# Attention with rational scores: new places for norm, block end and queries, and another instruction order in key tiles 23 to 31

## The chip, the cores and the metric

The kernel runs on one core of one Trainium2 chip. The metric is the device time of one execution in microseconds (us), the median over repeated runs. Five engines work side by side, each in its own order: TensorE (PE, matrix products into PSUM), VectorE (DVE), ScalarE (ACT, functions such as logarithm and exponential), GpSimd (POOL) and SyncE (SP, which issues DMA transfers). [...]

## The reference

The input x is 4 x 128 x 64 x 64. A first layer (group norm, convolutions, a selective scan) adds its result to x; the change does not touch it. The second layer treats each of the four images as 4096 tokens of 128 channels, normalises each token, and adds an additive attention; a recurrent layer follows. The attention is:

```python
q = jnp.einsum('bld,ud->blu', x, Wt)
k = jnp.einsum('bld,ud->blu', x, Wx)
beta = jnp.tanh(q[:, :, None, :] + k[:, None, :, :] + bh)
alpha = jnp.einsum('bsju,u->bsj', beta, Wa[:, 0]) + ba[0]
alpha = jnp.tanh(alpha)
alpha = jax.nn.softmax(alpha, axis=-1)
c_r = jnp.einsum('bsj,bjd->bsd', alpha, x)
```

So every query meets every key through 32 hyperbolic tangents, weighted by Wa and summed.

## The kernel before

The stage in question is `_rational`. It doesn't evaluate 32 tangents for each pair of query and key. The 32 units are put into six small groups, and the weighted sum of the tangents of one group is a quotient of two sums over products of exponentials. Both sums are matrix products of a table for the keys, F, with a table for the queries, E (lower sum, the denominator) or cE (upper sum, the numerator). The tables are exponentials of projections (`keys`, `queries`; `weigh` makes cE from E).

**Tiles and blocks.** For each of the 4 batches (images) there are 8 query blocks of 512 queries, 32 blocks in all. Within a block the loop runs over 32 key tiles of 128 keys, number jt. A tile's scores go to A[:, jt, :], 128 keys by 512 queries. When all tiles of a block are there, a seam follows: tanh and exp over A in four parts (PARTS), the first weighted sums over the values (`weighted`, accumulated in one PSUM bank, `ct`), and tile 0 of the next block, computed ahead without ScalarE (`ahead`, `direct`, with VectorE's reciprocal). So all blocks but the first start their loop at tile 1. Where a batch ends, the next batch's key table is made in the seam as well (`all_keys`), and the transposed values (`turn`, eight of them) in the loop of the block that follows.

**One tile.** The six groups are served as three units, A, B1 and B2, of two groups each. Each unit needs:
- d: the lower sums, two matmuls into two PSUM banks (`lower`; called dA, dB1, dB2 here; two buffers of two banks in all). A uses rows 0 to 63 and 64 to 127 of TensorE, B1 rows 0 to 31 and 32 to 63, B2 rows 64 to 95 and 96 to 127.
- n: the upper sums, two matmuls into two numerators' banks (`upper`; nA, nB1, nB2).
- ln and ex: ScalarE takes the logarithm of the lower sums and then the exponential of its negative, which gives the reciprocals (lines 1231 and 1232).
- x: VectorE multiplies them with the upper sums, one multiply for each bank (`times`, line 1227).

Then POOL adds the products of B1 to those of A (a1, line 1349) and those of B2 (a2, line 1334), and VectorE adds the two halves of the result into A (f, line 1346). n and x of B2, a2 and f of a tile are issued in the next tile's iteration. The products of A live in the pool `ra` (three buffers), those of B1 and B2 in the pool `rb` (four buffers of one unit).

**Order.** Each engine is handed its instructions in the order in which the Python code issues them. In one iteration TensorE gets dA(jt), nB2(jt-1), dB1(jt), nA(jt), dB2(jt), nB1(jt); ScalarE ln and ex of A, B1 and B2 in turn; VectorE xB2(jt-1), xA(jt), xB1(jt), f(jt-1); POOL a2(jt-1), a1(jt).

**Extra steps.** Other work is put between the tiles by number: `between[jt]` runs at the end of iteration jt, `middle[jt]` within it, after a2.
- The last 12 weighted sums of the block before run in `middle`, tiles 2 to 13.
- The end of the block before (`closing`) has seven steps at CLOSE_AT: the copy of `ct` to SBUF, a matmul for the softmax denominators, four quarter reciprocals, and the last step: a matmul, a VectorE multiply, a POOL add to the residual `xr` (line 1264) and the store on SP.
- The norm of a part of the next batch has four steps at NORM_AT: centre (matmul, VectorE subtract), square (ScalarE), rate (matmul, ScalarE ln and exp, lines 71 and 72) and scale (POOL multiply, line 1164). The blocks of batches 0 to 2 have it, those of the fourth batch do not.
- The two halves of the next block's query table come at QUERIES_AT: a matmul, an exponential, and a maximum on VectorE.

PSUM holds two buffers for the lower sums (four banks), three numerators' banks (`pn`, taken in turn; also used by turns and the norm), and one bank `ct` for the weighted sum, the block end and the queries (`pw`).

## Time and profile before

| | |
|---|---|
| median of 3 runs | 11600.68 us (11594.8 to 11604.92) |
| the profiled execution's own time | 11599.52 us |
| its span, first to last instruction | 11597.8 us |
| granted TensorE clock, mean | 0.935 |
| busy share PE, DVE, ACT, POOL | 89%, 78%, 82%, 74% |
| first ScalarE table load of the attention loop, and the last one that follows a seam | 4001.83 us, 11137.38 us |
| a1, a2, f: mean of one | 2656 ns, 2362 ns, 749 ns |

A row of a group or of the timeline names the line of the program, the engine, the operation, the tile written and the tiles read, and the shape as partitions by elements. In the timeline the two numbers ahead are start and duration in us; what stands in brackets at the end is how long the engine was idle before, and what ended that. `pd` are the banks of the lower sums, `pn` those of the upper sums, `ra` and `rb` the products. A matmul in fp32 has two records (passes), so a unit of two matmuls has four. PEld is the loading of weights.

### The profile page before, as it was taken

How to read it: one execution, taken by the hardware profiler on the slowest of the kernel's cores; microseconds unless marked ns; L12 is line 12 of the kernel's file. 1: busy time of each engine (PE TensorE's matmuls, PEld its weight loads, DVE VectorE, ACT ScalarE, POOL GpSimd, SP SyncE). 2: the span in 40 equal slices, each digit the busy share in tenths (PEclk: the TensorE clock that was granted, in tenths of full speed). 3: DMA queues.
4: the chain of work that ended last, by engine and by line, in shares of the span. 5: the costliest groups of instructions: out<-in, count | busy, mean ns of one | idle time of the engine just before them, and what ended most of it. 6: DMA issues, size and time to landing. Idle time of an engine off the chain costs nothing.

```text
span 11597.8 us, 111820 instructions
## 1 busy us (share of the span) xinstructions
PE 10265.4 (89%) x36210; PEld 3139.3 (27%) x36210; DVE 8992.9 (78%) x10066; ACT 9467.7 (82%) x10209; POOL 8626.5 (74%) x3703
## 2 busy tenths in 40 slices
PE   6787787778777699999999999999999999999997
PEld 2121121122111132232233223323323233333334
DVE  4998899889889677777777777777777777777773
ACT  3556656656555599999999999999999999999995
POOL 3999889889889677767766776767677767776773
PEclk8898898888888799999999999999999999999998
DMA  4888778778778300000000000000000000000001
GB/s 118 189 182 195 169 179 192 178 173 190 180 169 194 85 1 3 6 3 4 6 3 3 3 6 3 3 3 6 3 3 3 6 2 3 3 4 3 2 3 60
DMA packets 225333, 737.77 MB, mean 64 GB/s; under 512 B 41105, under 2 KB 41937, under 8 KB 223713
## 3 DMA queue, kind: packets, MB, share of 16 engines
q1 hardware_dynamic: 221760, 729.96, 26.7%
q8 instruction: 286, 4.69, 0.2%
q14 instruction: 311, 2.54, 0.1%
q10 hardware_dynamic: 2976, 0.58, 0.0%
HBM read 612.95 MB, written 117.44 MB: 63 GB/s over the span
## 4 chain that ended last, share of the span: by engine, by line
PE 50%; ACT 10%; DVE 3%; issue 3%; POOL 0%; DMA 0%; POOLq 0%; DVEq 0%; SPq 0%; ACTq 0%
PE pn L1212 26%; PE pd L1212 16%; PE ct L1360 4%; ACT A L1384 4%; ACT A L1385 2%; DVE rb L1227 2%; ACT rb L1231 1%; ACT rb L1232 1%; PE ct L1134 1%; ACT ra L1231 1%; PE vy L1559 1%; DVE A L1346 0%; PE ct L1262 0%; PE pn L56 0%; ACT L1384 0%
## 5 line engine op out<-in xcount | busy, mean ns | idle before, releaser
L1212 PE MATMUL pn<-cE,F 32*128 32x512 f32 (+1 forms) x12288 | 4691.2, 651 | 189.9 <-DVE rb L1227 86.0
L1212 PE MATMUL pd<-E,F 32*128 32x512 f32 (+1 forms) x12288 | 3481.5, 649 | 20.4 <-DVE ra L1239 15.5
L1349 POOL TENSOR_TENSOR ra<-ra,rb 128x1024 f32<-128x1024 f32 x993 | 2637.0, 2656 | 1077.5 <-DVE rb L1227 1077.3
L1227 DVE TENSOR_TENSOR rb<-rb,pn 128x512 f32<-128x512 f32 x3972 | 2566.0, 681 | 960.0 <-ACT rb L1232 369.5
L626 POOL TENSOR_TENSOR dBu<-dtdu,bbcc 128x1024 f32<-128x1024 f32 x1024 | 2397.9, 2367 | 217.8 <-DMA dtdu<-ddd 158.8
L1334 POOL TENSOR_TENSOR ra<-ra,rb 128x1024 f32<-128x1024 f32 x993 | 2345.6, 2362 | 228.4 <-DVE rb L1227 123.9
L1232 ACT ACTIVATE rb<-rb 128x1024 f32<-128x1024 f32 x1986 | 2099.5, 1057 | 62.9
L1231 ACT ACTIVATE rb<-pd 128x1024 f32<-128x1024 f32 x1986 | 2004.6, 1009 | 112.5 <-PE pn L1212 84.9
L1212 PEld LDWEIGHTS pn<-cE,F 32*128 32x128 f32 (+1 forms) x12288 | 1367.1, 186 | 2553.9 <-DVE rb L1227 1386.2
L668 PE MATMUL py<-h,gather 128*32 128x512 f32 x4096 | 1300.7, 701 | 471.3 <-POOL h L651 359.7
L1227 DVE TENSOR_TENSOR ra<-ra,pn 128x512 f32<-128x512 f32 x1986 | 1288.2, 683 | 528.1 <-PE pn L1212 325.0
L1212 PEld LDWEIGHTS pd<-E,F 32*128 32x128 f32 (+1 forms) x12288 | 933.2, 186 | 1646.9 <-issue 820.7
L621 ACT ACTIVATE pa<-dtdu,a_neg 128x1024 f32<-128x1024 f32 x1024 | 1145.2, 1118 | 53.1 <-DVE h L641 32.1
L651 POOL TENSOR_TENSOR h<-h,bbcc 128x1024 f32<-128x1024 f32 x384 | 911.7, 2374 | 346.0 <-ACT carry L649 336.5
L641 DVE TENSOR_TENSOR_SCAN pa<-pa,carry,dBu 128x1024 f32<-128x1024 f32 x480 | 1124.5, 2343 | 23.1 <-ACT pa L621 11.3
L1232 ACT ACTIVATE ra<-ra 128x1024 f32<-128x1024 f32 x993 | 1049.7, 1057 | 31.4
L1360 PE MATMUL ct<-A,xT 128*128 128x512 f32 x2048 | 1052.3, 642 | 8.8 <-ACT A L1385 8.8
L1231 ACT ACTIVATE ra<-pd 128x1024 f32<-128x1024 f32 x993 | 1001.3, 1008 | 31.7 <-PE pd L1212 26.4
L649 ACT COPY carry<-pa 128x1 f32<-128x1 f32 x640 | 102.5, 160 | 1044.2 <-DVE h L648 1042.2
L1346 DVE TENSOR_TENSOR A<-ra 128x512 f32<-128x512 f32 x993 | 743.3, 749 | 115.9 <-POOL ra L1334 115.8
L648 DVE TENSOR_TENSOR h<-pa,bbcc 128x1024 f32<-128x1024 f32 x640 | 783.8, 1225 | 59.0 <-PE py L668 0.9
L641 DVE TENSOR_TENSOR_SCAN h<-pa,carry,dBu 128x1024 f32<-128x1024 f32 x288 | 675.0, 2344 | 171.0 <-PE py L668 141.1
(291 smaller groups left out, 8740.9 us busy)
## 6 DMA issues: line engine op xcount, KB each, us to landing
bbcc<-bcd SPq DMA_DIRECT2D x1024, 256.0 KB, 6.9
dtdu<-ddd SPq DMA_DIRECT2D x1024, 256.0 KB, 7.2
ddd<-dd SPq DMA_DIRECT2D x64, 1024.0 KB, 5.1
src<-src SPq DMA_DIRECT2D x64, 512.0 KB, 8.3
xs<-in_x_dram SPq DMA_DIRECT2D x16, 512.0 KB, 7.5
src<-xs SPq DMA_DIRECT2D x16, 512.0 KB, 3.0
bcd<-bc SPq DMA_DIRECT2D x64, 128.0 KB, 2.0
src<-xsT SPq DMA_DIRECT2D x16, 512.0 KB, 5.4
```

What stands on the lines that cost most here:

```text
L621: nc.scalar.activation(dA, its[m].DT[r][:, 0, :], AF.Exp, scale=a)
L626: nc.gpsimd.tensor_tensor(dBu, its[m].DT[r][:, 1, :], its[m].BC[q][:, 0, :], ALU.mult)
L641: nc.vector.tensor_tensor_scan(to[:, step], dA[:, step], live.pop(("dBu", u))[:, step], 0.0 if m % nch == 0 else its[m - 1].carry[:, col : ...
L651: nc.gpsimd.tensor_tensor(h, h, cc, ALU.mult)
L668: nc.tensor.matmul(it.y[to, c], gather, live["h", v][:, c], start=False, stop=(q == QS - 1))
L1212: nc.tensor.matmul(ps[a], F[lo:hi, i, jt * P : (jt + 1) * P], side[lo:hi, i, :], start=True, stop=True)
L1227: nc.vector.tensor_tensor(r[:, a, :], r[:, a, :], ns[a], ALU.mult)
L1231: nc.scalar.activation(r, d, AF.Ln, scale=LOWER)
L1232: nc.scalar.activation(r, r, AF.Exp, scale=-1.0)
L1334: nc.gpsimd.tensor_tensor(rA_, rA_, rB2_, ALU.add)
L1349: nc.gpsimd.tensor_tensor(rA, rA, rB1, ALU.add)
L1360: nc.tensor.matmul(ct, xT[:, jt, :], A[:, jt, :], start=(jt == 0), stop=(jt == JT - 1))
```

## The change

Every step of a tile gets a number of its own, and all steps of a block, with the extra steps, are sorted by number and issued in that order. For tiles up to 22 the numbers (EARLY_STEPS) give the order from before. From tile 23 on (LATE_STEPS) they give another one: ScalarE runs lnA, lnB1, exA, lnB2 and then one exponential over B1 and B2 together (exB, 128 x 2048); TensorE runs, from tile to tile, nB1(jt-1), dB2(jt), nB2(jt-1), dA(jt+1), nA(jt), dB1(jt+1); VectorE xB1(jt-1), f(jt-2), xB2(jt-1), xA(jt); POOL a1(jt-1), a2(jt-1).

For that, the products of B1 and B2 share one buffer of the pool `rb` (now three buffers of two units). The bank that was `ct` becomes the fourth of the numerators' banks from tile 23 on; up to there three are taken in turn as before, and the fourth serves weighted sum, block end, queries and, newly, the rate of the norm. The extra steps all end before: block end at tiles 13 to 18, norm at 14 to 20, queries at the ends of tiles 20 and 21. The norm's square is kept in the A tile of key tile 31, which is free then; the exponential of the rate is written to the PSUM bank, and the scale is a VectorE multiply that reads it there, where it was a POOL multiply. The sums f of tiles 30 and 31 are issued in the seam, behind the first `direct` of the next block's tile 0.

```diff
-CLOSE_AT = (14, 16, 17, 18, 19, 20, 22)
-NORM_AT = (15, 17, 19, 20)
-QUERIES_AT = (24, 26)
+LATE = 23
+CLOSE_AT = (13.45, 14.45, 14.95, 15.95, 16.95, 17.95, 18.95)
+NORM_AT = (14.95, 16.95, 19.95, 20.45)
+QUERIES_AT = (20.95, 21.95)
+EARLY_STEPS = dict(
+    dA=0.00, dB1=0.10, nA=0.20, lnA=0.21, exA=0.22, xA=0.23, dB2=0.30, nB1=0.31, lnB1=0.40, exB1=0.41,
+    xB1=0.42, a1=0.44, lnB2=0.50, exB2=0.51, nB2=1.05, xB2=1.12, a2=1.13, f=1.43,
+)
+LATE_STEPS = dict(
+    dA=-0.44, dB1=-0.23, lnA=-0.12, lnB1=-0.04, exA=0.26, dB2=0.37, lnB2=0.50, nA=0.74, xA=0.81, exB=0.84,
+    nB1=1.11, xB1=1.38, nB2=1.42, xB2=1.49, a1=1.75, a2=1.88, f=2.46,
+)
...
-    rb = ctx.enter_context(tc.tile_pool(name="nrb", bufs=4))
+    rb = ctx.enter_context(tc.tile_pool(name="nrb", bufs=3))
-    psN = ctx.enter_context(tc.tile_pool(name="npsN", bufs=3, space=PSUM))
-    psW = ctx.enter_context(tc.tile_pool(name="npsW", bufs=1, space=PSUM))
+    psN = ctx.enter_context(tc.tile_pool(name="npsN", bufs=1, space=PSUM))
...
+    turns = {"taken": 0, "banks": 3}
     def pn():
-        return psN.tile([P, QB], F32, name="pn", tag="pn")
+        i = turns["taken"] % turns["banks"]
+        turns["taken"] += 1
+        return psN.tile([P, QB], F32, name=f"pn{i}", tag=f"pn{i}")
     def pw():
-        return psW.tile([P, QB], F32, name="ct", tag="ct")
+        return psN.tile([P, QB], F32, name="pn3", tag="pn3")
...
+    def norm_within(xn, cols, A):
...
+        def square():
+            nc.scalar.activation(A[:, JT - 1, :], xc, AF.Square)
+        def rate():
+            held["ps"] = ps = pw()
+            nc.tensor.matmul(ps, k.avg, A[:, JT - 1, :], start=True, stop=True)
+            nc.scalar.activation(A[:, JT - 1, :], ps, AF.Ln, bias=k.eps5)
+            nc.scalar.activation(ps, A[:, JT - 1, :], AF.Exp, scale=-0.5)
+        def scale():
+            nc.vector.tensor_tensor(xc, xc, held["ps"], ALU.mult)
...
+    def four():
+        return rb.tile([P, 4, QB], F32, name="rb", tag="rb")
+    def pair():
+        return ra.tile([P, 2, QB], F32, name="ra", tag="ra")
+    def steps(jt, F, E, cE, A, first):
...
+        when = EARLY_STEPS if jt < LATE else LATE_STEPS
...
+        if jt >= LATE:
+            go["exB"] = lambda: exp(h["rb"])
+        else:
+            go["exB1"] = lambda: exp(halves("B1"))
+            go["exB2"] = lambda: exp(halves("B2"))
...
+        return [(jt + when[name] + (JT if name == "f" and jt >= JT - 2 else 0), f) for name, f in go.items()]
...
+            between.append((LATE - 0.05, lambda: turns.update(banks=4)))
+            for jt in range(start, JT):
+                between += steps(jt, F, E, cE, A, first if jt == start else None)
+            between.sort(key=lambda e: e[0])
+            for _, go in between[:-2]:
+                go()
+            sums = [go for _, go in between[-2:]] if more else []
...
                 if step == 0:
-                    held["A"], held["B1"] = lower("A", F, 0, E), lower("B1", F, 0, E)
-                    held["A"] = direct(held["A"], upper("A", F, 0, cE), ra, "ra")
+                    dA, held["dB1"] = lower("A", F, 0, E), lower("B1", F, 0, E)
+                    held["A"], held["B"] = pair(), four()
+                    direct(held["A"], dA, upper("A", F, 0, cE))
+                    for go in sums:
+                        go()
...
-                    between.setdefault(22 + c, []).append(lambda xT=xT, xn=xn, c=c: turn(xT, xn, c))
+                    between.append((21.85 + c, lambda xT=xT, xn=xn, c=c: turn(xT, xn, c)))
```

## The prediction

> **What bounds the kernel now.** I read the page's busy shares first, then the stretches by engine, then the timeline of single tiles. The attention stage runs from 4044 to about 11378 us: 32 query blocks of 31 key tiles (32 in the first), a seam after each.

> ```profile
> PE 10265.4 (89%) x36210; PEld 3139.3 (27%) x36210; DVE 8992.9 (78%) x10066; ACT 9467.7 (82%) x10209; POOL 8626.5 (74%) x3703
> L1231 ACT ACTIVATE rb<-pd 128x1024 f32<-128x1024 f32 x1986 | 2004.6, 1009 | 112.5 <-PE pn L1212 84.9
> L1231 ACT ACTIVATE ra<-pd 128x1024 f32<-128x1024 f32 x993 | 1001.3, 1008 | 31.7 <-PE pd L1212 26.4
> ```

> The second and third rows are the logarithms; what follows the second bar is idle time of ScalarE before them. Next, two stretches: one whole block without its seam, and three tiles in it.

> ```profile
> 6350.98:6548.66 197.68, 194.08 (x777) 58.23 (x776) 145.29 (x225) 188.99 (x192) 155.88 (x64) 0.98 0.01 5
> 6475.00:6496.50 21.50, 19.20 (x70) 5.43 (x69) 15.92 (x23) 16.53 (x18) 15.31 (x8) 0.84 0.03 10
> ```

> Columns are PE, PEld, DVE, ACT, POOL and the granted clock. ScalarE is busy 189.0 of 197.7 us in the block, yet 16.5 of 21.5 in the three tiles. So ScalarE sets the pace except in one place. Its pace in an undisturbed tile:

> ```profile
> 6074.71 1.00 ACT L1231 ACTIVATE ra<-pd 128x1024 f32<-128x1024 f32 x1
> 6075.75 1.06 ACT L1232 ACTIVATE ra<-ra 128x1024 f32<-128x1024 f32 x1
> 6076.71 1.00 ACT L1231 ACTIVATE rb<-pd 128x1024 f32<-128x1024 f32 x1
> 6080.72 1.00 ACT L1231 ACTIVATE ra<-pd 128x1024 f32<-128x1024 f32 x1
> 6096.16 1.91 ACT L1385 ACTIVATE A<-A 128x2048 f32<-128x2048 f32 x1
> 6097.97 3.69 ACT L1384 ACTIVATE A<-A,b_a 128x4096 f32<-128x4096 f32 x1
> ```

> A tile is 6.00 us (6074.71 to 6080.72). An exponential starts 1.04 after the logarithm it needs (1.00 long); the next, independent instruction starts 0.96 after the exponential (1.06 long). Independence is worth an overlap of 0.09, dependence costs 0.04. The 2048-wide exponential takes 1.91, its successor starts after 1.81.

> The bad place, first how a good tile looks, then a block's tile 21 to 22:

> ```profile
> 6007.16 0.70 PE L1212 MATMUL pn<-cE,F 32*128 32x512 f32 x2
> 6007.24 0.70 PE L1212 MATMUL pd<-E,F 32*128 32x512 f32 x2
> 6007.51 0.69 DVE L1346 TENSOR_TENSOR A<-ra 128x512 f32<-128x512 f32 x1
> 6007.69 0.59 PE L1212 MATMUL pn<-cE,F 32*128 32x512 f32 x2
> 6007.73 2.68 POOL L1349 TENSOR_TENSOR ra<-ra,rb 128x1024 f32<-128x1024 f32 x1 [1.49 <-DVE rb L1227]
> 6010.49 2.36 POOL L1334 TENSOR_TENSOR ra<-ra,rb 128x1024 f32<-128x1024 f32 x1
> ...
> 6482.27 2.35 POOL L1349 TENSOR_TENSOR ra<-ra,rb 128x1024 f32<-128x1024 f32 x1
> 6482.35 2.81 DVE L1346 TENSOR_TENSOR A<-ra 128x512 f32<-128x512 f32 x1 [0.42 <-POOL ra L1334]
> 6485.82 1.85 PE L1212 MATMUL pn<-cE,F 64*128 64x512 f32 x2 [2.06 <-DVE rb L1227]
> 6489.78 1.02 ACT L1231 ACTIVATE rb<-pd 128x1024 f32<-128x1024 f32 x1 [3.17 <-PE pn L1212]
> 6493.42 1.02 ACT L1231 ACTIVATE ra<-pd 128x1024 f32<-128x1024 f32 x1 [1.53 <-PE pd L1212]
> ```

> In the good tile f (L1346) starts 0.22 before the POOL add a1 and takes 0.69. In the bad one a1 starts 0.08 before f, and f takes 2.81: it ends 0.54 after a1 does. xB2 is queued behind f, the numerators' banks behind xB2, TensorE behind the banks. TensorE idles 2.06, its next pair takes 1.85 where such a pair takes 1.12 (clock 0.84 in that stretch), and ScalarE loses 3.17 + 1.53 = 4.70. The cause stands a tile earlier: POOL's scale of the norm (L1164, 1.27 us) comes between a1 and a2, so a2 ends late and a1 follows at once.

> **Part 1, tiles 23 to 31 (LATE_STEPS).** ScalarE's order becomes lnA, lnB1, exA, lnB2, exB, with one 2048-wide exponential. Start to start: lnA 0.92, lnB1 0.92, exA 0.97 (each with the overlap), lnB2 1.03 (exB needs it), exB 1.82: 5.66 instead of 6.00. Do the others keep up? Put lnA(j) at 0.
> - TensorE. A unit of two matmuls takes 1.06 (6006.10 to 7.16). Now nB2+dB1 and dB2+nB1 run as pairs on different row groups, four slots a tile. In the new order dB2, nB2, dA, nA, dB1, nB1, equal row groups follow each other, and only nB1 with the next dB2 can overlap. dB2 waits for lnA (1.01), so dB2 at 1.1, nB2 2.16, dA 3.22, nA 4.28, dB1 5.34 to 6.40; lnB1 of the next tile wants it at 6.58: 0.18 to spare. Own loop: 5 x 1.06 + 0.08 = 5.38.
> - VectorE: six multiplies and f, at 0.64 and 0.6 apart: 4.5. xA follows nA (5.34), xB1 nB1 (7.45 to 8.7), then f, xB2 9.35 to 10.6.
> - POOL: from the end of xB1, 0.22 + 2.68 + 0.08 + 2.36 = 5.34 to the end of a2; the next f is safe if that is under the period: 0.32 to spare (0.66 now).
> - Four numerators' banks: nA reuses those of nB1(j-1), free at 8.7 - 5.66 = 3.0, before 4.28. Three fours of rb live until a2, 13.9, against reuse at 17.9. No wait.

> I take 5.70, for one handover of 0.04. In three blocks turns stand in these tiles (one more PE slot of 0.7, so 6.0: no gain). 29 x 9 x 0.30 = 78 us. Bounds: ScalarE with every overlap, 3 x 1.01 + 1.06 + 1.91 - 5 x 0.09 = 5.55 (117 us); below that nothing in the rows allows.

> The order on TensorE deserves a look. In the rows above, dB1's first pass starts 0.08 after nB2's while nB2's second pass waits until 0.53: a later matmul on free row groups passes waiting ones. [...]

> **Part 2, tiles 13 to 22.** Take, denominator, reciprocals, end, norm and queries move up; each issues the same matmuls, activations and VectorE work as before, and the ScalarE part (square 0.54, rate 1.24, two E of 0.5) costs the same elsewhere. On SP the end's store stands ahead of the next block's xr and xn loads (6495.19, 6497.19, 6497.56); all three come four tiles earlier and are needed 20 tiles later. Scale leaves POOL: 1.27 gone there, 0.68 more on VectorE (the row of a multiply with a PSUM operand), which has a quarter of its time free. Without that cover it would cost 24 x 0.68 = 16. The exponential of the rate writes PSUM: 0.63 before; no row shows that direction, 0.5 to 0.7 either way is 24 x 0.1 = 2 us, taken as 0.

> The end's POOL add (1.27) remains. It alone also makes f lose, as the fourth batch shows, whose blocks have no norm: f took 2.85 at 9936.00 and ScalarE lost 2.29. After the change the add is at 18.95 in every block. In the 24 blocks with a norm, the rate's 1.24 us on ScalarE and one matmul follow a tile later, at 19.95, just where f is blocked: the 2.2 us delay of xB2 meets ScalarE 1.24 later, and TensorE idles 0.7 (1.78 before the row at 9939.51, less the rate's 1.06). I keep 0.5 per block (bounds 0 and 2.3, from 2.29).
> Total of the stall now: 84.9 + 26.4 = 111. Fourth batch: 8 x 2.29 = 18, stays. The rest, 93, becomes 24 x 0.5 = 12: gain 81.

> **Part 3, the seam.** f(30) and f(31) move behind the first direct reciprocals. ScalarE fills 31.7 us there (table load 6092.83 to lnA at 6124.54) with tanh and exponentials; the last tanh needs f(31) 19.6 after the load. xB2(31) ends 2.6 after it, weigh 0.9, direct 8.1, two f 1.3: 13. Cost 0; without this cover 31 x 1.3 = 40. Tiles 1 to 12 keep their order: 0.

> **Sum**, against the profiled execution (11599.5, span 11597.8; median of the runs 11600.7): 11599.5 - 78 - 81 = 11440.

> **Rivals.**
> 1. The stall only changes its cause: the end's add does in each block what the scale did, f 2.8 long, TensorE slow. For it: the fourth batch. Against: there no rate follows. Only part 1 is left: 11599.5 - 78 = 11521.
> 2. TensorE becomes the bound in the late tiles: no overlap at all, 6 x 1.06 = 6.36 a tile; 261 x 0.36 = +94, less 81: 11612. For: three numerators of four now stand behind an equal row group. Against: the 0.08 above.
> 3. Slower: POOL loses the race in tiles 23 to 31. From the point where a1 and a2 need more than the period (0.32 away), f is blocked in each tile: f 2.85, xB2 1.28, a2 2.36, handovers: 6.55 a tile, and the gain of the shorter exponential cannot be used. 261 x 0.55 = +144, less 81: 11662. Against: a blocked f delays xA and xB1 too, which lets POOL catch up, and VectorE's other multiplies (0.68 beside POOL) don't collide.

> **How the numbers follow.** Forecast 0.68, rival 1 0.18, rival 2 0.06, rival 3 0.08. Range: low end 11599.5 - 117 - 93 = 11390, a little under it for the rows' rounding, 11380; high end rival 1 with the slower late tile (44): 11555, taken as 11545. About 0.2% (23 us) is what a measurement can tell. Faster: forecast and rival 1, 0.86; within: rival 2, 0.06; slower: rival 3, 0.08.

> **What would show it.** Distance of lnA in tiles 23 to 30: 5.7; over 5.8 with waits on PE speaks for rival 2. Mean of f (0.749 now): near 0.70 if the collisions go; over 0.9 is rival 3. Idle of the logarithms on PE (111 now): near 30; if it stays over 90, rival 1. I am wrong if the seam waits for f(31), or tiles 13 to 22 take over 66 us where they take 67.6 now.

## The result and the profile after

The changed kernel takes 11759.92 us (median of 4 runs, 11746.45 to 11775.18), the kernel before 11602.8 in the same comparison (4 runs, 11594.8 to 11605.37): a ratio of 1.0138, 95% interval 1.0124 to 1.0151. The forecast was 11440. The profiled execution took 11746.45 us (span 11744.6), 147 more than the profiled one of before; the mean granted clock of TensorE is 0.926 (0.935 before).

The page of the changed kernel, rows that answer to those shown of before; `log` is now line 1271, a1, a2 and f are 1324, 1325 and 1326:

```profile
PE 10260.4 (87%) x36210; PEld 3244.2 (28%) x36210; DVE 9285.6 (79%) x10090; ACT 9411.6 (80%) x9921; POOL 8552.1 (73%) x3679
L1324 POOL TENSOR_TENSOR ra<-ra,rb 128x1024 f32<-128x1024 f32 x993 | 2590.8, 2609 | 1032.0 <-DVE rb L1268 959.2
L1271 ACT ACTIVATE rb<-pd 128x1024 f32<-128x1024 f32 x1986 | 2016.2, 1015 | 203.6 <-PE pd L1253 143.1
L1271 ACT ACTIVATE ra<-pd 128x1024 f32<-128x1024 f32 x993 | 1003.1, 1010 | 112.8 <-PE pd L1253 72.3
L1326 DVE TENSOR_TENSOR A<-ra 128x512 f32<-128x512 f32 x993 | 931.5, 941 | 140.0 <-POOL ra L1325 140.0
```

ScalarE does 56 us less work (9467.7 to 9411.6: the shorter exponentials). Its idle before the logarithms should have fallen from 144 us (112.5 + 31.7) to about 30; it rose to 316 (203.6 + 112.8), most of it on the lower sums of TensorE. The mean of f went from 749 to 941 ns.

Where the 147 us lie follows from the starts of lnA in the timeline of ScalarE. A tile is the distance of two of them; the last tile ends, and the seam begins, with the load of tanh's table. Sums over the 32 blocks, profiled executions, in us:

```
                     before    after   difference
tiles 1 to 12        2364.2   2452.4     +88.2    of it tile 1: 6.02 -> 8.4 each; tiles 2 to 4: 6.00 -> 6.20
tiles 13 to 22       2088.6   2155.4     +66.8    tile 22: 10.07 -> 6.01; tile 20: 6.00 -> 9.88; tile 14: 6.05 -> 7.15
tiles 23 to 31       1786.6   1778.5      -8.1    11 blocks of 50.7, 18 of 56 to 61
seams                 999.1   1000.6      +1.5
```

(The single tiles are means over 21 blocks of batches 0 to 2: all but the first of each batch.) So all three stretches miss the forecast, which had -78 for tiles 23 to 31, -81 for the stalls, whose steps move into tiles 13 to 22, and 0 for the seam and the tiles behind it. The -8 of tiles 23 to 31 is a sum of large parts that the experiments separate: the queries' leaving (-55), the late order with the clock kept up (-104), and a loss of 150.

**Tiles 23 to 31.** Two blocks in the view of stretches; columns are PE, PEld, DVE, ACT, POOL, the granted clock:

```profile
4429.50:4490.30 60.80, 56.77 (x211) 20.78 (x206) 45.56 (x61) 51.32 (x46) 40.67 (x17) 0.83 0.00 0
4902.10:4952.90 50.80, 49.67 (x213) 17.94 (x207) 37.50 (x61) 50.51 (x46) 42.54 (x18) 1.00 0.00 1
```

The second is as forecast: ScalarE busy throughout, 5.62 us a tile (forecast 5.70). In the first, with the same work, TensorE's clock is 0.83 and it takes 10 us more. Its timeline from the fourth late tile on, POOL and VectorE's f:

```profile
4451.93 2.37 POOL L1324 TENSOR_TENSOR ra<-ra,rb 128x1024 f32<-128x1024 f32 x1
4452.02 2.82 DVE L1326 TENSOR_TENSOR A<-ra 128x512 f32<-128x512 f32 x1 [0.84 <-POOL ra L1325]
4456.18 2.37 POOL L1325 TENSOR_TENSOR ra<-ra,rb 128x1024 f32<-128x1024 f32 x1 [1.89 <-DVE rb L1268]
4458.57 2.35 POOL L1324 TENSOR_TENSOR ra<-ra,rb 128x1024 f32<-128x1024 f32 x1
4458.59 2.89 DVE L1326 TENSOR_TENSOR A<-ra 128x512 f32<-128x512 f32 x1 [0.16 <-POOL ra L1325]
4462.82 2.37 POOL L1325 TENSOR_TENSOR ra<-ra,rb 128x1024 f32<-128x1024 f32 x1 [1.89 <-DVE rb L1268]
4465.21 2.35 POOL L1324 TENSOR_TENSOR ra<-ra,rb 128x1024 f32<-128x1024 f32 x1
```

This is the loop of the third rival: f waits for a2, a1 starts 0.02 to 0.09 before f, f takes 2.82 to 2.89, xB2 follows f, a2 follows xB2, 6.64 us a tile (a1 from 4458.57 to 4465.21). What starts it stands in the views below: the clock.

**Tiles 13 to 22.** The block of the second row, around tile 20:

```profile
4877.51 2.35 POOL L1324 TENSOR_TENSOR ra<-ra,rb 128x1024 f32<-128x1024 f32 x1
4877.56 2.86 DVE L1326 TENSOR_TENSOR A<-ra 128x512 f32<-128x512 f32 x1 [0.19 <-POOL ra L1325]
4878.69 0.60 ACT L1202 ACTIVATE pn<-A 128x512 f32<-128x512 f32 x1
4885.21 0.68 DVE L1205 TENSOR_TENSOR xn<-xn,pn 128x512 f32<-128x512 f32 x1
4885.95 1.12 PE L1150 MATMUL pn<-xn,w_q 128*128 128x512 f32 x2 [2.56 <-DVE xn L1205]
4888.69 1.02 ACT L1271 ACTIVATE ra<-pd 128x1024 f32<-128x1024 f32 x1 [0.99 <-PE pd L1253]
```

The first two rows are the collision of before, two tiles earlier, behind the end's POOL add. The next three are new: the queries' matmul (line 1150) waits 2.56 us for the scale (line 1205). It reads nothing that the scale writes in this block; both use the fourth bank. The rate's exponential now lies there (third row), and the bank is free only when scale has read it. The next tile's lower sums stand behind the queries on TensorE.

**Tile 1.** The seam ahead of the same block, and the start of its tile 1; first the changed kernel, then the kernel before at the same place:

```profile
4726.03 1.28 ACT L1455 ACT_TABLE_LOAD   x1
4728.62 2.35 POOL L1324 TENSOR_TENSOR ra<-ra,rb 128x1024 f32<-128x1024 f32 x1
4728.69 5.07 DVE L1241 TENSOR_SCALAR cE<-E,c_n 128x512 f32<-128x512 f32 x2
4731.05 2.42 POOL L1325 TENSOR_TENSOR ra<-ra,rb 128x1024 f32<-128x1024 f32 x1
4733.68 3.35 DVE L1279 RECIPROCAL ra<-pd 128x512 f32<-128x512 f32 x1
4741.80 1.29 DVE L1326 TENSOR_TENSOR A<-ra 128x512 f32<-128x512 f32 x2
4757.74 1.02 ACT L1271 ACTIVATE ra<-pd 128x1024 f32<-128x1024 f32 x1
4758.64 0.69 DVE L1280 SCALAR_TENSOR_TENSOR rb<-rb,pn 128x512 f32<-128x512 f32 x1
4760.82 1.02 ACT L1271 ACTIVATE rb<-pd 128x1024 f32<-128x1024 f32 x1 [0.97 <-PE pd L1253]
```

```profile
4709.18 1.28 ACT L1384 ACT_TABLE_LOAD   x1
4713.75 0.69 DVE L1346 TENSOR_TENSOR A<-ra 128x512 f32<-128x512 f32 x1 [3.27 <-POOL ra L1334]
4714.36 0.88 DVE L1200 TENSOR_SCALAR cE<-E,c_n 128x512 f32<-128x512 f32 x2
4715.15 3.35 DVE L1239 RECIPROCAL ra<-pd 128x512 f32<-128x512 f32 x1
4738.89 0.69 DVE L1240 SCALAR_TENSOR_TENSOR rb<-rb,pn 128x512 f32<-128x512 f32 x1
4740.89 1.02 ACT L1231 ACTIVATE ra<-pd 128x1024 f32<-128x1024 f32 x1
```

Before, VectorE waited 3.27 for f(31), and POOL was done when `weigh` came: cE took 0.88. Now `weigh` runs into POOL's a1 and a2 of tile 31 and takes 5.07. The first direct reciprocal starts 7.65 after the table load (5.97 before), and f(30), f(31) add 1.29: the chain on VectorE is 3.0 later. Its last multiply comes 0.90 after the start of lnA(1) (4758.64, 4757.74) instead of 2.00 before it (4738.89, 4740.89), and ScalarE waits in tile 1 for lower sums (0.97).

### The profile page after: what moved, and what is told of

It is laid out like the page before. It is cut to its first block, busy times and chain, and to the rows that moved or that the text cites. A ratio compares the mean times of both kernels' runs of the same rounds, so it can differ in the third digit from the quotient of the medians.

```text
span 11744.6 us, 109361 instructions
## 1 busy us (share of the span) xinstructions
PE 10260.4 (87%) x36210; PEld 3244.2 (28%) x36210; DVE 9285.6 (79%) x10090; ACT 9411.6 (80%) x9921; POOL 8552.1 (73%) x3679
## 4 chain that ended last, share of the span: by engine, by line
PE 41%; DVE 10%; ACT 10%; issue 4%; POOL 2%; DMA 0%; DVEq 0%; POOLq 0%; SPq 0%; ACTq 0%
PE pn L1253 19%; PE pd L1253 13%; PE pn L1426 6%; ACT rb L1271 4%; DVE rb L1268 3%; ACT ra L1271 2%; ACT ra L1274 2%; DVE ra L1279 2%; DVE rb L1279 2%; DVE A L1326 1%; ACT rb L1274 1%; DVE cE L1241 1%; POOL ra L1325 1%; POOL ra L1324 1%; PE pn L1150 1%
## 5 line engine op out<-in xcount | busy, mean ns | idle before, releaser
L1253 PE MATMUL pn<-cE,F 32*128 32x512 f32 (+1 forms) x12288 | 4242.1, 651 | 133.0 <-DVE rb L1268 105.4
L1271 ACT ACTIVATE rb<-pd 128x1024 f32<-128x1024 f32 x1986 | 2016.2, 1015 | 203.6 <-PE pd L1253 143.1
L1274 ACT ACTIVATE rb<-rb 128x1024 f32<-128x1024 f32 (+1 forms) x1698 | 2040.9, 1202 | 54.0
L1271 ACT ACTIVATE ra<-pd 128x1024 f32<-128x1024 f32 x993 | 1003.1, 1010 | 112.8 <-PE pd L1253 72.3
L1426 PE MATMUL pn<-A,xT 128*128 128x512 f32 x2048 | 1057.4, 645 | 7.6 <-ACT A L1456 7.6
L1326 DVE TENSOR_TENSOR A<-ra 128x512 f32<-128x512 f32 x993 | 931.5, 941 | 140.0 <-POOL ra L1325 140.0
```

What stands on the lines that cost most here:

```text
L1253: nc.tensor.matmul(ps[a], F[lo:hi, i, jt * P : (jt + 1) * P], side[lo:hi, i, :], start=True, stop=True)
L1271: nc.scalar.activation(r, d, AF.Ln, scale=LOWER)
L1274: nc.scalar.activation(r, r, AF.Exp, scale=-1.0)
L1326: go["f"] = lambda: nc.vector.tensor_tensor(A[:, jt, :], h["ra"][:, 0, :], h["ra"][:, 1, :], ALU.add)
L1426: nc.tensor.matmul(ct, xT[:, jt, :], A[:, jt, :], start=(jt == 0), stop=(jt == JT - 1))
```

## The experiments

Each one is the changed kernel with the edit shown; times are of one execution, beside 11595 to 11602 of the kernel before, except where an interval stands. Since the number of long blocks in tiles 23 to 31 varies by itself, I read each experiment in the stretch that it aims at. All runs in one table (sums over 32 blocks; tiles 1 and 20 are means of 21 blocks with a norm; "low" is the time at half clock in tiles 23 to 31, from the clock's record):

```
              time     1 to 12  13 to 22  23 to 31    low   blocks >=56   tile 1  tile 20
before      11599.5     2364      2089      1787       34        6         6.02     6.00
after       11746.5     2452      2155      1778      296       18         8.36     9.88
e1_seam     11810.3     2437      2183      1826      402       27         8.50    10.39
e2_end      11783.3     2481      2153      1787      307       25         9.95    10.69
e3_pairs    12095.1     2505      2160      2022      569       32        10.31    10.02
e5_noadd    11629.1     2414      2187      1670      116        0         7.03    10.91
e6_order    11641.9     2443      2194      1644       27        1         7.92    11.27
e7_scale    11619.1     2454      2099      1709      154       10         8.52     8.14
e8_weigh    11752.2     2431      2190      1768      290       20         7.82    11.13
e9_three    11628.6     2403      2125      1740      246        7         6.63     9.01
e11_alt     11619.8     2443      2185      1628        3        0         7.98    11.03
e13_early   11631.7     2372      2168      1732       10        0         6.05    10.15
e12_best    11431.6     2407      2040      1632       13        1         6.62     6.48
e14_centre  11418.9     2409      2029      1628        0        0         6.86     6.48
```

(Of e12_best and e14_centre the table has the profiled run, as of all; their medians stand below.)

### First attempts, one for each theory

**e1_seam.** In the seam, the reciprocals of unit A come before `weigh`; cE, the upper sums and the products follow the first weighted sums.

```diff
-                E, cE = E_next, weigh(E_next)
+                E = E_next
...
-                    direct(held["A"], dA, upper("A", F, 0, cE))
+                    for a in range(2):
+                        nc.vector.reciprocal(held["A"][:, a, :], dA[:, a, :])
...
+                if more and i == 0:
+                    cE = weigh(E)
+                    ahead(0.5)
```

> Edit: in the seam the two reciprocals of unit A run before the scaling that makes cE, and the first weighted sums before the matmuls that read cE. Theory: in the changed kernel the scaling (SBUF to SBUF, mean 2393 ns against 479 before) is blocked by POOL's last two adds, and the reciprocal chain ends too late for tile 1. Behind 6.7 us of reciprocals POOL is done: scaling near 0.5 us, tile 1 from a mean of 8.3 back to 6.0, tiles 1 to 12 from a mean of 76.6 to 73.6, the kernel about 88 us shorter, 11660. Rival (tile 1 waits for buffers, three of rb instead of four): tile 1 stays above 8, the time at 11740.

Measured: 11810.3. cE is short (436 ns each, 2336 in the changed kernel), yet tile 1 takes 8.50. In block 3 (counted from 0, the block of the timelines above) the reciprocal now waits for dA, which TensorE reaches late at half clock, and nA stands behind weighted sums. Around the start of that seam half clock lasts 17 us. Ahead of block 27 it lasts only 7 there, and tile 1 took 6.02. So the collision of cE isn't the whole of tile 1; TensorE's clock at the end of the block is the other part.

**e2_end.** The end's add on VectorE with a PSUM operand.

```diff
-            nc.vector.tensor_tensor(held["rec"], held["rec"], num, ALU.mult)
-            nc.gpsimd.tensor_tensor(xr, xr, held["rec"], ALU.add)
+            nc.vector.tensor_tensor(num, held["rec"], num, ALU.mult)
+            nc.vector.tensor_tensor(xr, xr, num, ALU.add)
```

> Edit: the block end's last add runs on VectorE and reads the product from PSUM, so POOL has only a1 and a2. Theory: the stall at tile 20 (mean 9.9 with a norm, 9.0 without) is f blocked because the end's POOL add delays a2. Then tile 20 falls to 6.0 to 6.3, tile 21 to 6.5, together about 110 us, the kernel near 11635. Rival (the crowd of extra steps, or the rate in PSUM, causes it): tile 20 stays above 8 and the time above 11700.

Measured: tile 20 falls from 8.97 to 6.48 in the last batch, which has no norm, and stays at 10.69 in the blocks with one. Taking out the add alone helps only where no norm is; with a norm something else holds tile 20 too. The wait for the bank above is the candidate.

**e3_pairs.** nB2 of the late tiles paired with another unit (a miss).

```diff
-    nB1=1.11, xB1=1.38, nB2=1.42, xB2=1.49, a1=1.75, a2=1.88, f=2.46,
+    nB1=1.11, xB1=1.38, nB2=1.78, xB2=1.82, a1=1.75, a2=1.88, f=2.46,
```

> Edit: in tiles 23 to 31 nB2 moves from 1.42 to 1.78 and xB2 from 1.49 to 1.82, so that dB2 stands next to nB1 and nB2 next to dB1 of other row groups: four slots of TensorE a tile in place of nearly six. [...] With pairs the clock stays full: each block without turns takes 50.7 to 51.5 us for tiles 23 to 31 (now 50.7 in some, 56 to 61 in most), about 140 us less, 11605. Rival (POOL loses the race against f by itself): f stays at 2.8 in many late tiles and the blocks at 56 to 61; the time at 11740.

Measured: 12095.1, every block long, 7.75 us a tile. xB2 now stands behind xA, so the loop of f, four multiplies and a2 is 2.82 + 4 x 0.62 + 2.35 = 7.65, with handovers 7.75: again the loop of rival 3, closed for good. Here it needs no help from the clock: in 21 of the 32 blocks the first f over 2 us comes before any half clock of the late tiles. The edit left the four B units of TensorE next to each other (dB1, nB2, nB1, dB2).

**e5_noadd.** a1 and a2 of tiles 23 to 30 are left out: does the clock fall without the collision?

```diff
+        if jt < LATE or jt == JT - 1:
             go["a1"] = lambda: nc.gpsimd.tensor_tensor(h["ra"], h["ra"], halves("B1"), ALU.add)
             go["a2"] = lambda: nc.gpsimd.tensor_tensor(h["ra"], h["ra"], halves("B2"), ALU.add)
```

> Edit: in tiles 23 to 30 POOL's two adds are left out, so the scores of these tiles miss the products of B1 and B2. f then cannot be blocked there. Theory (clock gate): many blocks still take 56 us or more for tiles 23 to 31, with halved clock, and only f's part of the loss goes. Rival (POOL race): all blocks without turns come to 50.7, about 140 us less.

Measured: 1670 us in tiles 23 to 31, most blocks at 51.9, f 754 ns. So the adds carry most of the loss. But tile 25 still takes 6.83 in the blocks with a norm, always beside one stretch of 3.4 us at half clock. So the clock falls without any collision. In the changed kernel it also comes first: in each of the 18 long blocks half clock begins 7.1 to 9.0 us after the start of tile 23, and the first f over 2 us 20.8 to 22.5 us after it; the 11 blocks of 50.7 have neither.

### What the clock follows

In the profiles of before and of the changed kernel the clock's record has two values, 1.00 and 0.50, and all its changes lie whole multiples of 3.413 us apart. Two such stretches of the changed kernel, two of a long block (the first row of the two blocks above) and one of the short block, all around the start of tile 24:

```profile
4433.48:4436.90 3.42, 2.75 (x14) 1.15 (x14) 2.70 (x5) 3.42 (x3) 0.69 (x1) 1.00 0.00 0
4436.90:4440.31 3.41, 3.41 (x10) 0.93 (x10) 1.36 (x3) 3.38 (x4) 2.35 (x1) 0.50 0.00 0
...
4907.97:4911.38 3.41, 2.74 (x14) 1.06 (x14) 2.49 (x5) 3.41 (x4) 1.28 (x1) 1.00 0.00 0
```

TensorE is busy for 2.75 and 2.74 us. After the first the clock is 0.50, after the third row's stretch it stayed full. What differs is how many rows the matmuls use: their records name 32, 64 or 128 (32\*128, 64\*128, 128\*128). Weighting the time of each matmul (its record less 0.16 us, by which a first pass of 0.69 runs on past the start of the second, 0.53 later) with its rows over 128 gives 0.37 in the first stretch and 0.45 in the other. A unit of B is two matmuls of 32 rows, a unit of A two of 64. The same sum, my own count from the records of the matmuls and of the clock, for every stretch between 4300 and 11200 us in five profiles:

```
            full, then half:       full, stays full:     half, then full:   half, stays half:
            number median highest  number lowest 5%      number lowest      number median highest
before         57    .18    .41     1854    < .52          57     .90         54    .62    .92
after         101    .38    .45     1725    < .48         101     .85         95    .70    .88
e9_three       67    .38    .45     1782    < .53          67     .90        105    .76    .92
e11_alt        72    .37    .45     1831    < .52          72     .90         47    .66    .91
e12_best       31    .35    .46     1936    < .52          31     .84         24    .73    .91
```

The share of time with any matmul doesn't separate them: in the changed kernel stretches of up to 0.93 were followed by half clock. (The bounds aren't sharp: some stretches of 0.38 to 0.45 stayed full, some of 0.84 to 0.92 stayed at half.) The lowest use before a way back was 0.84 (e12_best) to 0.90 (before). Two stretches of one block of e9_three:

```profile
4425.08:4428.49 3.41, 2.74 (x13) 0.98 (x12) 2.52 (x5) 3.41 (x3) 0.86 (x1) 1.00 0.00 0
...
4438.73:4442.14 3.41, 3.41 (x8) 1.00 (x8) 1.89 (x3) 3.38 (x3) 1.33 (x1) 0.50 0.00 0
```

TensorE has no idle time in the second one, and the clock remains at half: its weighted use is 0.76, and that block stays at half for eleven stretches in a row, 9.7 us a tile.

The two bounds can be read as one; this is an estimate from the same records. In the changed kernel dA takes 2.08 at half clock (4439.24) and 1.13 at full clock (4445.58), about twice as long, so a use of 0.84 to 0.92 at half clock is about the work of 0.42 to 0.46 at full clock, where the falls lie too (up to 0.46). With the use at half clock halved, of the about 10,100 stretches of the five runs none above 0.46 is followed by half clock and none under 0.38 by full clock; the 430 between go either way. This is a count over the records of this case; no run was made to test it by itself.

In the order of the change four units of B follow each other (dB1, nB1, dB2, nB2), 0.96 apart, and in tile 24 dB2 waits 0.7 for lnA: 4.5 us with at most 64 rows in use, longer than a stretch of 3.413. How much of a stretch falls into them depends on its phase, and the long and the short blocks divide by it: in the 29 blocks without turns, all 11 whose tile 23 starts 0.08 to 1.24 or 3.40 us behind an edge of the clock's record are short, and all 18 that start 1.29 to 3.10 behind one are long.

**e6_order and e11_alt** change only where dA and dB1 are issued in the late tiles, and with it how many B units stand together: three with the 0.7 idle (3.6 us), then two (2.6 us).

```diff
-    dA=-0.44, dB1=-0.23, lnA=-0.12, ...
+    dA=-0.595, dB1=-0.23, lnA=-0.12, ...      (e6_order)
+    dA=-0.595, dB1=-0.27, lnA=-0.12, ...      (e11_alt)
```

> Edit: in tiles 23 to 31 the lower sums dA of the next tile are issued before nB2 instead of after it (dA -0.595 in place of -0.44), so that TensorE's order per tile is nB1, dB2, dA, nB2, nA, dB1 and at most three units that fill half the array follow each other, where dB1, nB1, dB2, nB2 are four now. Nothing else is changed. Theory 'gate': the granted clock halves in a late tile because a clock window falls into four half-array units in a row; with the edit the low-clock time in the late tiles (296 us over 32 blocks in the changed kernel) falls under 100 us, most blocks take 50 to 52 us for tiles 23 to 31 where 17 of 32 take 56 or more now, and the time is 11746 - 150 = about 11600 (range 11580 to 11660). Theory 'POOL race' alone (f blocked by a1, TensorE's order without weight): low-clock time and the number of slow blocks stay as they are, 11740 to 11790, or worse, since xB2 comes 1 us later and a2 with it.

> Edit: dA of the next tile ahead of nB2, and dB1 of the next tile ahead of nA, in tiles 23 to 31 (dA -0.595, dB1 -0.27 in place of -0.44, -0.23): TensorE's order per tile is dB2, dA, nB2, dB1, nA, nB1, so at most two half-array units follow each other, where e6_order leaves three (dB1, nB1, dB2). Theory 'gate' (the clock falls when the array's use, weighted by the rows of each matmul, is under 0.43 to 0.45 in a window of 3.4 us, and comes back only over about 0.9): two halves and an idle of 0.75 still give 0.50, so no late tile falls to the low clock; low-clock time in the late tiles under 10 us (27 in e6_order, one block of 62.6 us), late sum 1630 to 1645, time 11620 to 11650. Rival: nA a unit later makes xA, xB1 and f late, tiles over 5.7.

Measured: half clock in tiles 23 to 31 goes from 296 to 27 and 3 us, long blocks from 18 to 1 and 0, the stretch from 1778 to 1644 and 1628. The same block 1 in e11_alt:

```profile
4431.70:4482.45 50.75, 49.62 (x211) 16.18 (x206) 37.20 (x61) 50.44 (x47) 42.24 (x17) 1.00 0.00 0
```

All of POOL's adds are there, and f takes 767 ns on the mean (941 in the changed kernel). In the late tiles 6 f take over 2 us, two in each of the three blocks with turns, against 85 in the changed kernel. So with the clock kept up POOL loses its race only beside the turns: in the change's order the clock starts the loss and the collision spreads it. e9_three shows that e6's order is not safe: another phase brought 7 long blocks, up to 67 us, without one f over 2 us. e11's order is: in e12_best and e14_centre, which share it, the starts of tile 23 lie all round the stretch (at most 0.26 apart), and all 58 blocks without turns take 50.7 or 50.8 us.

### The middle and the seam

**e7_scale.** The scale ahead of tile 20's multiplies, same banks.

```diff
-NORM_AT = (14.95, 16.95, 19.95, 20.45)
+NORM_AT = (14.95, 16.95, 19.95, 20.2)
```

> Edit: the norm's scale on VectorE is issued ahead of tile 20's multiplies (20.2 in place of 20.45), with the same banks and operands. Theory 'bank': the rate's result stays in the fourth bank until scale has read it, the queries' matmul waits for this bank on TensorE and the next tile's sums wait behind it; tile 20 in the blocks with a norm falls from 9.9 us to 6.4 to 7.2, and the sum of tiles 13 to 22 from 2155 to about 2085. Theory 'end's add' (the second way of the prediction: f blocked by the end's POOL add sets tile 20): tile 20 stays at 9 to 10 us. The total can hide this, since the number of slow blocks in tiles 23 to 31 varies by itself: 11640 to 11760 by the first, 11730 to 11790 by the second.

Measured: tile 20 in the blocks with a norm 8.14: 12 of 21 take 6.92, 9 take 9.77. In block 2, one of the nine:

```profile
4621.77 2.87 DVE L1326 TENSOR_TENSOR A<-ra 128x512 f32<-128x512 f32 x1 [0.18 <-POOL ra L1325]
4625.76 0.68 DVE L1205 TENSOR_TENSOR xn<-xn,pn 128x512 f32<-128x512 f32 x1
4629.09 2.08 PE L1150 MATMUL pn<-xn,w_q 128*128 128x512 f32 x2
```

The scale is done 2.6 before the queries start, so the bank no longer holds them. What remains is f behind the end's add (2.85 in block 1 too, one of the twelve), and in the nine blocks half clock after it (the queries take 2.08, 1.12 at full clock). Tiles 13 to 22 went to 2099, not to the 2085 expected.

**e8_weigh.** cE ahead of xB1(31) and xB2(31).

```diff
+            late = {}
+            if more:
+                between.append((JT + 0.425, lambda late=late, E_next=E_next: late.update(cE=weigh(E_next))))
...
-                E, cE = E_next, weigh(E_next)
+                E, cE = E_next, late["cE"]
...
-        return [(jt + when[name] + (JT if name == "f" and jt >= JT - 2 else 0), f) for name, f in go.items()]
+        return [(jt + when[name] + (JT if name == "f" and jt >= JT - 2 else 0.055 if name == "xB1" and jt == JT - 1 else 0), f) for name, f in go.items()]
```

> Edit: cE of the next block is made before xB1(31), xB2(31) on VectorE, so that a1(31) and a2(31) on POOL can't run beside it. Theory 'seam': the two cE instructions (2.34 us each in the changed kernel, 0.48 before) are blocked by POOL's last adds, and with f(30), f(31) they make the chain of direct reciprocals 3.0 us late, which tile 1 shows (8.4 against 6.0) and after it tiles 2 to 5 (6.2 against 6.0), because TensorE starts without a lead. Then cE falls under 1.2 us each, tile 1 under 7.3, the tiles 1 to 12 from 2452 to about 2405 us over the blocks. Rival: the two f alone (1.3 us) and TensorE's late numerators set tile 1; cE gets short and tile 1 stays over 8. Total 11690 to 11760 by the first, 11740 to 11790 by the second.

Measured: cE 648 ns each, tile 1 7.82: between theory and rival. **e9_three** puts e6, e7 and e8 together.

> The three edits together (order of dA in the late tiles, scale ahead of tile 20's multiplies, cE before the last multiplies). If the three causes are independent and add up: 11746 - 150 - 70 - 50 = 11480 (range 11440 to 11560), below the kernel before (11600). If the late tiles' slow state is chance that any shift of phase brings back, over 11600.

Measured: 11628.6, since the late tiles fell to half clock in other blocks. But tile 1 is 6.63, where either edit alone leaves 7.8 to 7.9: cE's collision and the clock at the block's end are both part of it.

**e13_early.** The late order switched off.

```diff
-LATE = 23
+LATE = 32
```

> Edit: the late order is switched off (LATE = 32): all tiles in the early order, everything else of the change kept (moved steps, rate in PSUM, three rings of rb, f(30) and f(31) behind the first direct reciprocals). Theory: the late order itself is not what costs the 147 us (tiles 23 to 31 took 1778 against 1787 before), the moved steps (tiles 13 to 22: +67) and the seam (tiles 1 to 12: +88) are: tiles 23 to 31 go to about 1780 to 1800, tiles 13 to 22 stay at 2130 to 2190, tile 1 gets shorter only as far as cE does; 11690 to 11770. Rival: late order and its clock cause the seam's delay too (TensorE at half clock when the block ends); then tile 1 goes back to 6.0 and the time to 11630 to 11670.

Measured: 11631.7, and the rival holds: tile 1 is 6.05 and tiles 1 to 12 take 2372. f(30) and f(31) behind the reciprocals cost nothing, as forecast, as long as the tiles before keep the early order; there the first reciprocal starts 4.5 after the table load although cE takes 3.35. The seam's loss belongs to the late order. That it does so because ScalarE ends its tile earlier there relative to VectorE and POOL is how I read the rows; no run tests it alone. My figure for tiles 23 to 31 was wrong: 1732, not 1780 to 1800, since the queries no longer stand in them (tiles 24 and 26 6.00 instead of 6.48; tile 24 took 8.87 in the last batch): 55 us of gain from the moved steps that I had booked nowhere.

### A version that beats both

**e12_best** joins e11's order, e7, e8 and e2.

> Four edits together: TensorE's order of e11_alt in the late tiles, scale ahead of tile 20's multiplies, cE before the last multiplies, and the end's add on VectorE with an operand in PSUM. If the causes add up: late tiles 1640 (gain 138 against the changed kernel's 1778), tiles 13 to 22 about 2050 (gain 105, tile 20 at 6.0 to 6.6 in all blocks), tiles 1 to 12 about 2400 (gain 50): 11746 - 293 = 11455, range 11430 to 11520, faster than the kernel before by 0.7 to 1.5%. If any shift of phase brings the low clock back as in e9_three (late 1740), 11550 to 11630.

Measured: 11427.94 (5 runs, 11422.16 to 11432.12), ratio to the kernel before 0.9848, interval 0.9835 to 0.9862. Tile 20 is 6.48 in 30 of the 32 blocks (6.63 in the first, 6.00 in the last, which has no queries), where e2_end alone leaves 10.69 and e7_scale alone 8.14: both causes had to go. Its page:

```profile
L1271 ACT ACTIVATE rb<-pd 128x1024 f32<-128x1024 f32 x1986 | 2014.8, 1015 | 54.0 <-PE pd L1253 11.3
L1271 ACT ACTIVATE ra<-pd 128x1024 f32<-128x1024 f32 x993 | 1001.3, 1008 | 32.3 <-PE pd L1253 27.0
L1326 DVE TENSOR_TENSOR A<-ra 128x512 f32<-128x512 f32 x993 | 691.4, 699 | 98.2 <-POOL ra L1325 98.2
```

The idle before the logarithms is 86 us, of 316 after the change and 144 before; f takes 699 ns. Tiles 1 to 12 still take 43 us more than before (2407, 2364); what holds them is open.

**e14_centre** moves the norm's centre one tile on.

```diff
-NORM_AT = (14.95, 16.95, 19.95, 20.2)
+NORM_AT = (15.95, 16.95, 19.95, 20.2)
```

> Edit on top of e12_best: the norm's centre one tile later (15.95 in place of 14.95), so that its matmul doesn't stand in the same tile as the block end's matmul for the denominators. Theory: moving steps isn't free, as the prediction had it ('costs the same elsewhere'): in tile 14 two matmuls of 1.06 each follow each other on TensorE, which has 0.3 us a tile to spare, and tile 14 takes 7.14 in the blocks with a norm (6.28 in those without, 6.05 before the change). Then tile 14 falls to about 6.3 and tile 15 rises by less (6.1 to 6.5): 24 blocks x 0.5 to 0.9, the time 11428 - 12 to 22 = 11406 to 11416. Rival: TensorE's work is the same and only shifts; tiles 14 to 16 keep their sum (19.76) and the time stays within 5 us of 11428.

Measured: 11418.95 (5 runs, 11417.66 to 11422.48), ratio 0.9846, interval 0.9832 to 0.9859. Tile 14 falls from 7.14 to 6.28, tiles 15 and 16 rise by 0.24 and 0.12: 0.5 a block are won, the rest only shifts. The tiles show this; the two ratios lie within each other's intervals.

## Why the prediction was wrong

- **Part 1, "Do the others keep up?"** ScalarE's pace was right (5.70 forecast, 5.62 measured; e13 to e11: 1732 - 1628 = 104 us, 78 forecast), and so was the overlap on TensorE against rival 2 (6.36 a tile without it). No run shows the 44 us of the range's high end (a slower late tile): with the clock kept up the late order gained those 104. The step that failed is TensorE's loop, "5 x 1.06 + 0.08 = 5.38": each 1.06 is a duration at full clock (the record of a unit in the changed kernel: 1.13, and 2.08 at half clock), and the sum asked only whether TensorE has time, not whether the new order keeps the clock. It didn't: 296 us of the late tiles ran at half clock (34 before). The trace of before had the rows (1.85 for a unit of 1.12, at 0.84), and I read them as a consequence of a stall.
- **Part 1, POOL "0.32 to spare".** True at full clock (e11_alt). In the long blocks rival 3's loop ran at 6.64 us (forecast 6.55). My condition for it was wrong: here a fallen clock brings it on and not POOL's own time, and the counter argument, that a blocked f lets POOL catch up, failed. Clock and collision together cost tiles 23 to 31 150 us (1778 - 1628); without the adds 108 of it go (e5_noadd, 1670).
- **Part 2, "the rate's 1.24 us" absorbs the block of f.** Failed: tile 20 took 9.88. Rival 1's collision came back (e2_end, last batch), and "the exponential of the rate writes PSUM ... taken as 0" priced an instruction but not the bank that it holds. I checked the numerators' banks for waits and not the fourth one. Both make TensorE wait, and the clock often falls behind them (e7_scale, nine of 21 blocks). The stall of tile 22 (4.07 a block) came back at tiles 20 and 21 (3.88 + 0.95).
- **Part 2, "costs the same elsewhere".** Failed in tile 14, where the centre now follows the block end's matmul: 1.1 a block, of which e14_centre gets 0.5 back. On the other side the queries' leaving of the late tiles gained 55 us, not booked.
- **Part 3, "Cost 0".** The seam itself costs nothing (+1.5 us). "Tiles 1 to 12 keep their order: 0" failed, at +88. I measured f(31) against its consumer, the last tanh, 19.6 after the load. The nearer deadline was the chain of reciprocals that it stands in, which was to end before lnA(1). The two f are 1.29 of the 3.0 by which that chain is late; in e13_early, where it starts earlier, they cost nothing. And "weigh 0.9" came from a row in which POOL was idle; beside a1 and a2 it took 5.07. I had named a wait of the seam as what would make me wrong, at the right place for the wrong reason; the other mark, 66 us for tiles 13 to 22, was passed with 68.3, a mean of 21 blocks with a norm (66.8 before; the prediction's 67.6 is one block).

f takes 2.82 where a1 started 0.09 earlier (4452.02, changed kernel) and ends 0.54 after it, and 0.68 where f was 0.23 ahead (4901.49). cE, which I had priced without POOL, takes 0.48 on the mean of before and 2.5 each behind a1 (two in 5.07, 4728.69), and the second ends 0.29 after a2. No row shows what holds f and cE in these places; the prices are those of the rows.

## What to carry to other kernels

Before reordering TensorE's work, list the array's rows of each matmul, and look for runs of small matmuls and idle time as long as one stretch of the clock's record (here 4.5 us against 3.413); spread the full ones between them (here half clock in the late tiles went from 296 to 3 us, e11_alt). When a result moves to PSUM, ask who takes the bank next, and until when its reader holds it (here the queries' matmul waited 2.56). And the deadline of a step that is moved is the next instruction on its own engine that is late, not its consumer alone.

## What was not expected of the hardware

Idle time alone doesn't tell the falls: of the 101 of the changed kernel between 4300 and 11200 us, 61 came after a stretch in which TensorE was never idle for more than 0.8 us, and 6 after a stretch that was nearly all idle.

Not tried: the moved steps with the old placement of the rate in SBUF, and the change's own order with full-array work added only to hold the clock.
